# Four column products instead of six taps' worth: the last sample's convolution on one core

## The chip, the cores and the metric

The kernel runs on one core of a Trainium2 chip. The metric is the device time of one execution in microseconds (us), the median of several runs. Engines are named as the profile names them: PE (matrix products), DVE and POOL (element work), ACT (functions, scaling and copies), SP (it issues most of the DMAs). PE's results go to PSUM[...]; the other tiles lie in SBUF, and whole images between the layers lie in DRAM.

## The reference, cut to what matters

Four samples of 128 channels, 128 x 128 pixels, fp32, pass four residual layers. Each adds to its input a function of the group-normalised input: a deformable convolution, a dilated convolution, a state-space block with four scan directions, and at the end the layer that the change is about:

```python
def _L3_conv_ref(x, W, b):               # x: (4,128,128,128), W: (128,128,3,3)
    norm_out = conv3x3(x, W, padding=1) + b[None, :, None, None]
    s = jnp.sum(x, axis=1, keepdims=True)
    p = jnp.pad(s, ((0,0),(0,0),(1,1),(1,1)), mode='edge')
    diff = p[:,:,:-2,1:-1] + p[:,:,2:,1:-1] + p[:,:,1:-1,:-2] + p[:,:,1:-1,2:] - 4.0*s
    return norm_out - 0.7 * diff
...
x = x + _L3_conv_ref(_gn(x), L3_conv_W, L3_conv_b)
```

The second term is a Laplacian of the channel sum. Its taps can be added to the 3 x 3 taps; what differs is the image's edge, where the convolution pads with zeros and the Laplacian repeats the edge pixel.

## The kernel before, in words

The samples are pipelined. A long main loop, `scan`, goes through 4 samples x 4 directions x 32 blocks of four image rows; beside it a generator called `side` is pulled along in step and issues the other layers of the neighbouring samples. Both write into the same instruction stream, and `keep_order` fixes each engine's order to the order in which the program issued the instructions. `together` runs the scan and its side work; what is left of the side work when the scan ends is issued by `drain`. For the last sample, the rest of layer 2 (`layer2_post`) is such side work: its last blocks can come only when the scan has summed its last direction. Last of all, `drain(layer3(sts[last]))` issues the fourth layer of the last sample, with nothing beside it.

`weave(n, order)` is a software pipeline. `order` is a list of groups of (delay, step); in round t each step is issued for item t - delay, groups in the order of the list. A step that is a generator gives one instruction at a time, at its own place and at each `MORE`.

`layer3` works on the image in strips of 8 rows (SB) and blocks of 4 rows, 512 pixels (N). It loads the nine tap matrices (`w_l_sb`), changes five of them on DVE for the Laplacian (L1219, L1220), fills one matrix `edge` with -0.7, and computes the group normalisation's scale and shift (`gn_affine`: L214 to L226). Then per strip: SP fetches 10 rows (tile `xr`, L1234), ACT normalises them in two halves (`xn`, L1243); per block: PE adds nine matmuls of up to 512 columns into one bank, and one-column or one-row matmuls with `edge` at the image's edge (`p`, L1264); DVE adds bias and input (`o`, L1271); SP stores the block (L146). Two banks take turns. Each matmul of the program has two records in the trace.

`layer2_post` ends with a chain per block on PE, ACT and POOL (L1113 to L1179), the statistics on DVE (`bn_stats`, L1184) and the store of the block to the DRAM image `x3d`. It goes through the blocks from the bottom of the image to the top.

Every tile belongs to a pool with a number of buffers. When a tile's buffer is used again, the first instructions on the new tile wait for the last ones on the old. Pools are stacked from the left or the right end of SBUF. The scan's three pools (`sch`, `scb`, `scp`, right) stay open to the end of the kernel.

Of the kernel before, what the change touches and what calls it, by code (L numbers as in the profile page):

```python
# [10 lines left out]
F32 = mybir.dt.float32  # L11
I32 = mybir.dt.int32
U32 = mybir.dt.uint32
AF = mybir.ActivationFunctionType
ALU = mybir.AluOpType
# [3 lines left out]
P = 128  # L19
H = 128  # L20
W = 128
HW = H * W
R = 4
N = R * W
NBLK = H // R
KK = 9
# [10 lines left out]
THETA = 0.7  # L37
# [4 lines left out]
SB = 8  # L42
# [4 lines left out]
V_PREW, V_PREB, V_POSTW, V_POSTB, V_CONVB, V_ONW, V_ONB, V_B3 = range(8)  # L47
# [25 lines left out]
def keep_order(tc, started):  # L73

    last = {}
    for ins in tc.nc.cur_bb.bb.instructions[started:]:
        before = last.get(ins.engine)
        if before is not None:
            tc.add_manual_dep(
                ins,  # L80
                before,
                mybir.DependencyInfo(mybir.DependencyClass.NoSync, mybir.DependencyReason.DATA),
                reason="in order",
            )
        last[ins.engine] = ins.name
# [5 lines left out]
def weave(n, order, ready=lambda t: True):  # L91


    total = n + max(step[0] for group in order for step in group if step is not MORE)
    for t in range(total):
        while not ready(t):
            yield None
        left = iter(())
        for k, group in enumerate(order):
            for step in group:  # L100
                if step is MORE:
                    next(left, None)
                elif 0 <= t - step[0] < n:
                    more = step[1](t - step[0])
                    left = left if more is None else more
            yield (t + (k + 1) / len(order)) / total
        for _ in left:
            pass
# [3 lines left out]
def conv_preact_kernel(ctx: ExitStack, tc: tile.TileContext, a: dict, nb: int):  # L112
    nc = tc.nc
    x_in, out = a["x"], a["out"]
# [4 lines left out]
    pss = ctx.enter_context(tc.tile_pool(name="scps", bufs=1, space=PSUM))  # L119
    psb = ctx.enter_context(tc.tile_pool(name="bgps", bufs=1, space=PSUM))  # L120

    def load(pool, src, shape, name, **kw):
        t = pool.tile(shape, F32, name=name, **kw)
        nc.sync.dma_start(t, src)
        return t

    def bank(which, name):
        return psb.tile([P, N], F32, name=name, tag=f"bank{which}")

    waiting = []  # L130
    beside = {}

    def store(dst, src, after=3, of=None):

        waiting.append([after, of, dst, src])
# [4 lines left out]
    def tick():  # L140
        for w in waiting:
            w[0] -= 1
        due = [w for w in waiting if w[0] <= 0]
        waiting[:] = [w for w in waiting if w[0] > 0]
        for w in due:
            nc.sync.dma_start(*w[2:])  # L146

    def flush():
        while waiting:
            nc.sync.dma_start(*waiting.pop(0)[2:])  # L150
# [14 lines left out]
    def col(i):  # L165
        return vec[:, i : i + 1]
# [32 lines left out]
    def rows_of(t, y, n):  # L199

        return t[:, y * W : (y + n) * W].rearrange("p (r w) -> p r w", w=W)

    def flat(t):
        return t.rearrange("p r w -> p (r w)")

    def rsqrt(dst, src, eps):
        nc.scalar.activation(dst, src, AF.Ln, bias=eps)
        nc.scalar.activation(dst, dst, AF.Exp, scale=-0.5)

    def gn_affine(stats, which=0):  # L210

        both = bank(which, "pmv")
        mv = small.tile([P, 2], F32, name="mv")
        nc.vector.bn_aggr(mv, stats)  # L214
        pm = both[:, 0:1]
        nc.tensor.matmul(pm, gmat, mv[:, 0:1], start=True, stop=True)
        d = small.tile([P, 1], F32, name="gnd")
        nc.vector.tensor_sub(d, mv[:, 0:1], pm)
        e = small.tile([P, 1], F32, name="gne")
        nc.vector.scalar_tensor_tensor(e, d, d, mv[:, 1:2], ALU.mult, ALU.add)  # L220
        pv = both[:, 1:2]
        nc.tensor.matmul(pv, gmat, e, start=True, stop=True)
        sc = small.tile([P, 1], F32, name="gnscale")
        rsqrt(sc, pv, gn_eps)
        sh = small.tile([P, 1], F32, name="gnshift")
        nc.vector.scalar_tensor_tensor(sh, pm, -1.0, sc, ALU.mult, ALU.mult)  # L226
        return sc, sh
# [562 lines left out]

    def scan(pull):

        hp = ctx.enter_context(tc.tile_pool(name="sch", bufs=5, side="right"))
        bp = ctx.enter_context(tc.tile_pool(name="scb", bufs=2, side="right"))
        sp = ctx.enter_context(tc.tile_pool(name="scp", bufs=2, side="right"))
        seq = []
        for st in sts:
            for k in (0, 1, 3, 2):
                back = k >= 2
                order = reversed(range(NBLK)) if back else range(NBLK)  # L800
# [139 lines left out]
        def finish(t):  # L940
            st, k, i, back = seq[t]
            y = sp.tile([P, N], F32, name="y", bufs=1)
            nc.scalar.copy(y, blocks[t]["y"])
            store(blk(st["y"][k % 2], i), y, of=st["y"])
            blocks[t] = None
            st["summed"] = t % (NDIR * NBLK) + 1 - 3 * NBLK
# [33 lines left out]
        for t, (st, k, i, back) in enumerate(seq):  # L980
            c = blocks[t]
# [5 lines left out]
            for g in range(NG):  # L987
# [7 lines left out]
                h, n = c["h", g], NG - 1 if ready else NG  # L995
# [8 lines left out]
                at = t * NST + g * NG  # L1004
# [8 lines left out]
                for ng in range(NG):  # L1013
                    n = g * NG + ng
# [26 lines left out]
                    o, f = h[:, ng, :], c["a", n]  # L1041
                    if back:
                        o, f = o[:, ::-1], f[:, ::-1]
# [6 lines left out]
        t = len(seq) - 1  # L1050
# [4 lines left out]
        sums(t, 3, 1)  # L1055
        finish(t)
        flush()


    def layer2_post(st, engine=nc.gpsimd):  # L1060
# [150 lines left out]
    def layer3(st):  # L1211
        x3d, stats = st["x3"], st["stats3"]
        ob = out[st["b"]].rearrange("c h w -> c (h w)")
        with ExitStack() as s:
# [63 lines left out]
            yield from weave(NBLK, order)  # L1278
            flush()

    def chain(parts):

        total = sum(w for _, w in parts)
        done = 0.0
        for stage, w in parts:
            for f in stage:
                yield None if f is None else (done + w * f) / total
            done += w
# [20 lines left out]
    def drain(gen):  # L1309
        for _ in gen:  # L1310
            tick()

    def together(main, side, share):

        at = 0.0

        def pull():
            nonlocal at
            f = next(side, 1.0)
            at = at if f is None else f  # L1320
            return f is not None

        for f in main(pull):
            while at < f * share and pull():
                pass
            tick()
        drain(side)

    sts = [{"b": b} for b in range(nb)]
    last = nb - 1  # L1330

    def loads(engine, stage, spare=False):
        for f in stage:
            beside["busy"], beside["spare"] = engine, spare
            yield f
        beside["busy"], beside["spare"] = None, False

    def head(b):
        st = sts[b]
        table = [(loads(None, layer0_table(st), True), 12)] if b < 2 else []  # L1340
        return table + [(loads("POOL", layer0(st)), 28), (loads("PE", layer1(st), True), 14),
                (loads("PE", layer2_pre(st), True), 36)]

    def tail(b):
        load = "PE" if b + 1 < last else None
        engine = nc.vector if load else nc.gpsimd
        post, conv = loads(load, layer2_post(sts[b], engine), True), layer3(sts[b])
        if b + 2 > last:
            return [(post, 16), (loads(load, conv, True), 22)]
        return [(post, 16), (loads(load, abreast(conv, layer0_table(sts[b + 2])), True), 34)]  # L1350

    first = head(0)
    ahead = layer0_table(sts[0], False)
    for f in layer0(sts[0]):
        tick()
        for _ in range(3):
            next(ahead, None)
            tick()
    drain(chain(first[2:-1]))
    begun = rest(first[-1][0], lambda: sts[0].get("out", 0) >= 4)  # L1360

    def around(b):

        side = [(begun, 18)] if b == 0 else tail(b - 1)
        if b < last:
            return side + head(b + 1)
        load, rounds = sum(w for _, w in side), NBLK + 10
        side = [(stage, (NDIR * NBLK + LATE - rounds) * w / load) for stage, w in side]
        return side + [(loads(None, layer2_post(sts[b]), True), rounds)]

    over = 1 + LATE / (NDIR * NBLK)
    side = chain([(chain(around(b)), over if b == last else 1) for b in range(nb)])
    together(scan, side, nb / (nb - 1 + over))
    drain(layer3(sts[last]))
    keep_order(tc, started)


# [81 lines left out]
```

## Time and profile before

| | |
|---|---|
| median of 3 runs | 21988.68 us (21982.39 to 22019.09) |
| the profiled execution's own time | 22048.69 us |
| its span, first to last instruction | 22046.9 us |
| busy over the span: PE, DVE, ACT, POOL | 80%, 81%, 74%, 80% |
| scan loop's DVE scans (L1044) | 8192 of 1.267 us |
| last convolution's PE instructions (L1264) | 21780.3 to 22042.9 us |

A row of the profile's groups names the line of the kernel, the engine, the operation, output and input tiles with their shapes, the count, the busy time and mean length of one, and the idle time just before with what ended it. The shares of busy time over the span say little about a change to one stage; for that one asks for a stretch of time alone. In the timeline, `SPq` rows are DMAs being issued, and the length there is the issue, not the transfer. `PEld` are weight loads.

### The profile page before, as it was taken

To read this page: it belongs to the slowest core of one execution; us is meant where nothing else is said; L and a number is where in the kernel's file an instruction comes from. 1 tells how busy PE (TensorE), PEld (TensorE's weight loads), DVE (VectorE), ACT (ScalarE), POOL (GpSimd) and SP (SyncE) were. 2 spreads that over 40 slices of the span, in tenths; PEclk is the share of its full clock that TensorE was granted. 3 is DMA by queue.
4 is the path that set the end of the run, shared out by engine and by line. 5 is a ranking of instruction groups with operands and counts; after the bars stand their busy time and mean duration, and the time that the engine had idled before them with its cause. 6 is when DMAs were issued, how large, how long until landed. Compare 5 with 4: busy or idle time off the path is not lost. (4 is left out here: it accounts for less than half of the span.)

```text
span 22046.9 us, 206313 instructions
## 1 busy us (share of the span) xinstructions
PE 17530.0 (80%) x51536; PEld 8506.2 (39%) x51536; DVE 17759.7 (81%) x18759; ACT 16420.1 (74%) x37439; POOL 17657.2 (80%) x11985
## 2 busy tenths in 40 slices
PE   4667777888878888788888887887887878778788
PEld 3444333445323333454533333344543333233333
DVE  2332688888998899888798889978889888999984
ACT  4775777888778776788868876688877877666673
POOL 3663787667899999777789999977779999999994
PEclk7888998999989999999999999999999999999999
DMA  7666678777766878777776697777776677556674
GB/s 226 189 187 185 191 241 274 245 242 246 255 207 221 237 242 266 243 246 243 246 249 216 219 262 240 257 245 240 250 252 219 221 224 228 200 202 209 214 233 134
DMA packets 2578940, 5040.76 MB, mean 229 GB/s; under 512 B 1060736, under 2 KB 1333576, under 8 KB 2435408
## 3 DMA queue, kind: packets, MB, share of 16 engines
q1 hardware_dynamic: 2209104, 3819.31, 53.2%
q0 software_dynamic: 368640, 1208.25, 18.1%
q8 instruction: 415, 6.80, 0.1%
q14 instruction: 781, 6.40, 0.1%
HBM read 4082.03 MB, written 874.52 MB: 225 GB/s over the span
## 5 line engine op out<-in xcount | busy, mean ns | idle before, releaser
L1044 DVE TENSOR_TENSOR_SCAN h<-pa,carry,h 128x512 f32<-128x512 f32 x8192 | 10011.3, 1267 | 605.7 <-ACT pa L919 386.4
L933 PE MATMUL yacc<-h,gather_sb 128*128 128x512 f32 x15264 | 7958.5, 648 | 1906.5 <-POOL h L959 1303.9
L959 POOL TENSOR_TENSOR h<-h,cb 128x1024 f32<-128x1024 f32 x3651 | 8589.1, 2365 | 622.3 <-ACT carry L953 575.2
L426 POOL DMA_INDIRECT g<-table,idx x4608 | 4535.8, 984 | 2470.2 <-issue 1174.3
L919 ACT ACTIVATE pa<-spread,neg_a 128x512 f32<-128x512 f32 x8192 | 5488.6, 682 | 109.9 <-DVE h L1044 82.3
L933 PEld LDWEIGHTS yacc<-h,gather_sb 128*128 128x128 f32 x15264 | 2967.8, 206 | 6073.5 <-issue 2925.7
L996 DVE TENSOR_TENSOR h<-dub,bb 128x2048 f32<-128x2048 f32 (+1 forms) x2048 | 4210.4, 2056 | 519.8 <-ACT dub L893 517.4
L464 PE MATMUL pst<-ident,g 128*128 128x128 f32 x9216 | 2134.8, 319 | 1327.6 <-ACT smp L469 1097.8
L440 ACT ACTIVATE g<-g,wt 128x128 f32<-128x128 f32 x9216 | 2839.4, 390 | 42.1 <-DMA g<-table,idx 38.9
L953 ACT COPY carry<-h 128x2 f32<-128x2 f32 x4096 | 769.5, 188 | 2705.7 <-DVE h L1044 2699.4
L464 PEld LDWEIGHTS pst<-ident,g 128*128 128x128 f32 x9216 | 1686.8, 224 | 2174.2 <-ACT smp L469 1614.3
L465 PE MATMUL pst<-ident,v 128*128 128x128 f32 x9216 | 2129.5, 318 | 321.9 <-DVE v L454 170.8
L451 DVE TENSOR_TENSOR pw<-pw,g 128x512 f32<-128x512 f32 x1152 | 797.0, 692 | 1961.2 <-ACT pw L440 1555.4
L465 PEld LDWEIGHTS pst<-ident,v 128*128 128x128 f32 x9216 | 1674.8, 227 | 419.2 <-DVE v L454 225.0
L440 ACT ACTIVATE pw<-g,wt 128x128 f32<-128x128 f32 x4608 | 1691.8, 367 | 131.7 <-DVE v L454 11.4
L893 ACT COPY dub<-spread 128x512 f32<-128x512 f32 x2048 | 1195.7, 584 | 302.4 <-DVE h L996 111.8
L454 DVE SCALAR_TENSOR_TENSOR v<-g,wt,pw 128x128 f32<-128x128 f32 x4608 | 1293.6, 343 | 114.4 <-issue 2.3
L475 PE MATMUL acc<-smp,w_sb 128*128 128x512 f32 x2304 | 1287.6, 642 | 21.4 <-DVE x L482 14.8
L469 ACT COPY smp<-pst 128x512 f32<-128x512 f32 x1152 | 668.1, 580 | 776.3 <-remote 578.2
L1264 PE MATMUL p<-xn,w_l_sb 128*128 128x508 f32 (+2 forms) x2304 | 1129.7, 608 | 1.8 <-ACT xn L1243 1.8
L899 POOL TENSOR_TENSOR h<-spread,bb 128x512 f32<-128x512 f32 x845 | 1079.5, 1278 | 15.9 <-DMA spread<-stepsd 10.2
L872 POOL TENSOR_TENSOR e<-e,one_e 128x512 f32<-128x512 f32 x423 | 538.2, 1272 | 486.8 <-ACT one_e L856 463.7
(183 smaller groups left out, 18935.7 us busy)
## 6 DMA issues: line engine op xcount, KB each, us to landing
spread<-stepsd SPq DMA_DIRECT2D x2048, 512.0 KB
bb<-bcd SPq DMA_DIRECT2D x512, 1024.0 KB
cb<-bcd SPq DMA_DIRECT2D x512, 1024.0 KB
stepsd<-steps SPq DMA_DIRECT2D x512, 512.0 KB
table<-gt SPq DMA_DIRECT2D x512, 256.0 KB
g<-table,idx POOLq DMA_INDIRECT x4608
u<-urow SPq DMA_DIRECT2D x256, 256.0 KB
yrow<-y SPq DMA_DIRECT2D x256, 256.0 KB
```

The lines of the kernel that those rows point to most:

```text
L426: nc.gpsimd.indirect_dma_start(out=g[:, r].rearrange("p q c -> p (q c)"), out_offset=None, in_=table, in_offset=bass.IndirectOffsetOnAxis( ...
L440: nc.scalar.activation(pw[:, r * P : (r + 1) * P] if c == 0 else g[:, r, c, :], g[:, r, c, :], AF.Copy, scale=wv[:, r, q, k, c : c + 1],)
L454: nc.vector.scalar_tensor_tensor(v[:, r, :], g[:, r, 3, :], wv[:, r, q, k, 3:4], pw[:, r, :], ALU.mult, ALU.add)
L464: nc.tensor.matmul(dst, g[:, r, 2, :], ident, start=True, stop=False)
L465: nc.tensor.matmul(dst, v[:, r, :], ident, start=False, stop=True)
L475: nc.tensor.matmul(got["a", i], w0[:, k, :], got.pop(("c", n)), start=k == 0, stop=k == KK - 1)
L893: nc.scalar.copy(p, blocks[t]["p", g][:, 1, :])
L919: nc.scalar.activation(pa, blocks[t]["p", g][:, 0, :], AF.Exp, scale=neg_a[:, k, n : n + 1])
L933: nc.tensor.matmul(c["y"], gather[:, g, :], c["h", g][:, ng, :], start=g == 0 and ng == 0, stop=last and ng == parts[-1] and not second,)
L959: engine.tensor_mul(h, h, c["cb"][:, 2 * half : 2 * half + 2, :])
L996: nc.vector.tensor_tensor(h[:, 0:n, :], c["pdu", g].unsqueeze(1).to_broadcast([P, n, N]), c["bb"][:, 0:n, :], ALU.mult)
L1044: nc.vector.tensor_tensor_scan(o, f, o, carry[:, n : n + 1], ALU.mult, ALU.add)
```

## The change

A new generator `last_layers` takes the place of `layer2_post` in the last sample's side work, and calls it; the separate `drain(layer3(...))` at the end goes. For the samples before the last nothing changes.

The convolution of a row with three taps (a, b, c) is done for two neighbouring output columns at a time. From four neighbouring input columns c0 to c3 four operands are formed: c0 - c2, c1 + c2, c2 - c1 and c1 - c3. With the tap matrices a, (a + b + c)/2, (a - b + c)/2 and c they give four products m0 to m3, and the two output columns are m0 + m1 + m2 and m1 - m2 - m3. Each product is for half of the columns, so 512 columns of a matmul now cover 8 rows, and a strip takes 4 products x 3 row taps instead of 2 blocks x 9 taps.

In detail:

- The strips are taken from the bottom up (`r`), in rounds of a strip instead of a block.
- `prepare` loads the taps and forms the four kinds of matrices on DVE, once: at the first step of `layer2_post` after the scan has ended (`beside["over"]`, set in `together`). Its pool, and later the strips' pool, lie on the right, where the scan's pools are now closed at the scan's end (`held`).
- `frame` sets the border columns and rows of `xn` to zero on POOL; `xn` has W + 2 columns and three buffers.
- `mix` forms the operands: two sums on DVE, two differences on POOL, 640 columns each, reading every second column.
- `multiply` issues the products in the order 1, 2, 0, 3 into four banks; odd strips use the side work's four banks, even strips those that the scan has left. The edge matmuls go with products 0 and 3 (m3 enters with a minus, so its matrix has +0.7).
- `combine` copies m1 to SBUF on ACT, forms each of the two columns on DVE with two instructions (bias included), adds the input on POOL into every second column of `o3`, and stores the whole strip.

```diff
@@ -790,9 +790,10 @@
     def scan(pull):
-        hp = ctx.enter_context(tc.tile_pool(name="sch", bufs=5, side="right"))
-        bp = ctx.enter_context(tc.tile_pool(name="scb", bufs=2, side="right"))
-        sp = ctx.enter_context(tc.tile_pool(name="scp", bufs=2, side="right"))
+        held = ExitStack()
+        hp = held.enter_context(tc.tile_pool(name="sch", bufs=5, side="right"))
+        bp = held.enter_context(tc.tile_pool(name="scb", bufs=2, side="right"))
+        sp = held.enter_context(tc.tile_pool(name="scp", bufs=2, side="right"))
         seq = []
         for st in sts:
             for k in (0, 1, 3, 2):
@@ -1055,6 +1056,7 @@
         sums(t, 3, 1)
         finish(t)
         flush()
+        held.close()
     def layer2_post(st, engine=nc.gpsimd):
@@ -1278,6 +1280,132 @@
             yield from weave(NBLK, order)
             flush()
+    def last_layers(st):
+        NSTR, WH = H // SB, W // 2
+        with ExitStack() as s:
+            def prepare():
+                wp = s.enter_context(tc.tile_pool(name="l3w", bufs=1, side="right"))
+                w = load(wp, a["w_l3"], [P, KK, P], "w_l3_sb")
+                for t in (1, 3, 5, 7):
+                    nc.vector.tensor_scalar_add(w[:, t, :], w[:, t, :], -THETA)
+                nc.vector.tensor_scalar_add(w[:, 4, :], w[:, 4, :], 4.0 * THETA)
+                w4 = w.rearrange("p (y x) c -> p y x c", x=3)
+                outer, middle, mixed = w4[:, :, 0, :], w4[:, :, 1, :], []
+                both = wp.tile([P, 3, P], F32, name="both")
+                nc.vector.tensor_add(both, outer, w4[:, :, 2, :])
+                for op in (ALU.add, ALU.subtract):
+                    m = wp.tile([P, 3, P], F32, name=f"mixed{len(mixed)}")
+                    nc.vector.tensor_tensor(m, both, middle, op)
+                    nc.vector.tensor_scalar_mul(m, m, 0.5)
+                    mixed.append(m)
+                weights = (outer, mixed[0], mixed[1], w4[:, :, 2, :])
+                edges = []
+                for v in (-THETA, THETA):
+                    edges.append(wp.tile([P, P], F32, name=f"edge{len(edges)}"))
+                    nc.vector.memset(edges[-1], v)
+                return weights, edges
+            made = None
+            for f in layer2_post(st):
+                if made is None and beside.get("over"):
+                    made = prepare()
+                yield f
+            weights, edges = made or prepare()
+            x3d, ob = st["x3"], out[st["b"]].rearrange("c h w -> c (h w)")
+            pp = s.enter_context(tc.tile_pool(name="l3p", bufs=2, side="right"))
+            sc, sh = gn_affine(st["stats3"])
+            got = {}
+            def r(what):
+                return lambda n: what(NSTR - 1 - n)
+            def inside(j):
+                return (1 if j == 0 else 0), (SB + 1 if j == NSTR - 1 else SB + 2)
+            def fetch(j):
+                lo, hi = inside(j)
+                got["x", j] = xr = pp.tile([P, SB + 2, W], F32, name="xr3", bufs=5)
+                nc.sync.dma_start(xr[:, lo:hi, :], rows_of(x3d, j * SB - 1 + lo, hi - lo))
+            def frame(j):
+                got["n", j] = xn = pp.tile([P, SB + 2, W + 2], F32, name="xn3", bufs=3)
+                for x in (0, W + 1):
+                    nc.gpsimd.memset(xn[:, :, x : x + 1], 0.0)
+                lo, hi = inside(j)
+                for y in (*range(0, lo), *range(hi, SB + 2)):
+                    nc.gpsimd.memset(xn[:, y : y + 1, :], 0.0)
+            def normalise(part):
+                def one(j):
+                    lo, hi = inside(j)
+                    o = slice(lo, SB // 2) if part == 0 else slice(SB // 2, hi)
+                    nc.scalar.activation(
+                        got["n", j][:, o, 1 : W + 1], got["x", j][:, o, :], AF.Identity, bias=sh, scale=sc
+                    )
+                return one
+            def mix(j):
+                xn = got["n", j]
+                got["v", j] = v = pp.tile([P, 4, SB + 2, WH], F32, name="v3")
+                c = [xn[:, :, k : k + W - 1 : 2] for k in range(4)]
+                nc.vector.tensor_add(v[:, 1], c[1], c[2])
+                nc.vector.tensor_sub(v[:, 2], c[2], c[1])
+                nc.gpsimd.tensor_sub(v[:, 0], c[0], c[2])
+                nc.gpsimd.tensor_sub(v[:, 3], c[1], c[3])
+            def multiply(j):
+                xn, v = got.pop(("n", j)), got.pop(("v", j))
+                if j % 2:
+                    m = [bank(k, "m3") for k in range(4)]
+                else:
+                    m = [pss.tile([P, N], F32, name="m3", tag=tag, bufs=bufs)
+                         for tag, bufs in (("pa", 2), ("pa", 2), ("dub", 1), ("yacc", 1))]
+                got["m", j] = m
+                rows = slice(1, SB + 1)
+                for k in (1, 2, 0, 3):
+                    p = m[k].rearrange("p (r w) -> p r w", w=WH)
+                    jobs = [(p, weights[k][:, ty, :], v[:, k, ty : ty + SB, :]) for ty in range(3)]
+                    if k in (0, 3):
+                        e, x, first = (edges[0], 0, 1) if k == 0 else (edges[1], WH - 1, 2)
+                        at = 1 if k == 0 else W
+                        jobs.append((p[:, :, x : x + 1], e, xn[:, rows, at : at + 1]))
+                        for y, edge_row in ((0, 0), (SB - 1, H - 1)):
+                            if j * SB + y == edge_row:
+                                jobs.append((p[:, y, :], e, xn[:, 1 + y, first : first + W - 1 : 2]))
+                    for n, (dst, wt, src) in enumerate(jobs):
+                        nc.tensor.matmul(dst, wt, src, start=n == 0, stop=n == len(jobs) - 1)
+            def combine(j):
+                m, xr = got.pop(("m", j)), got.pop(("x", j))
+                s1 = pp.tile([P, N], F32, name="s3")
+                nc.scalar.copy(s1, m[1])
+                o = pp.tile([P, SB, W], F32, name="o3")
+                for x, op in ((0, ALU.add), (1, ALU.subtract)):
+                    e = pp.tile([P, N], F32, name=f"e{x}")
+                    nc.vector.tensor_tensor(e, s1, m[2], op)
+                    if x == 0:
+                        nc.vector.scalar_tensor_tensor(e, m[0], col(V_B3), e, ALU.add, ALU.add)
+                    else:
+                        nc.vector.scalar_tensor_tensor(e, e, col(V_B3), m[3], ALU.add, ALU.subtract)
+                    nc.gpsimd.tensor_add(
+                        o[:, :, x:W:2], e.rearrange("p (r w) -> p r w", w=WH), xr[:, 1 : SB + 1, x:W:2]
+                    )
+                store(ob[:, j * SB * W : (j + 1) * SB * W], flat(o), after=1)
+            order = [[(0, r(fetch)), (1, r(frame))], [(2, r(normalise(0)))], [(2, r(normalise(1)))],
+                     [(3, r(mix))], [(4, r(multiply))], [(4, r(combine))]]
+            for _ in weave(NSTR, order):
+                yield 1.0
+            flush()
     def chain(parts):
         total = sum(w for _, w in parts)
@@ -1324,6 +1452,7 @@
             while at < f * share and pull():
                 pass
             tick()
+        beside["over"] = True
         drain(side)
     sts = [{"b": b} for b in range(nb)]
@@ -1366,12 +1495,11 @@
             return side + head(b + 1)
         load, rounds = sum(w for _, w in side), NBLK + 10
         side = [(stage, (NDIR * NBLK + LATE - rounds) * w / load) for stage, w in side]
-        return side + [(loads(None, layer2_post(sts[b]), True), rounds)]
+        return side + [(loads(None, last_layers(sts[b]), True), rounds)]
     over = 1 + LATE / (NDIR * NBLK)
     side = chain([(chain(around(b)), over if b == last else 1) for b in range(nb)])
     together(scan, side, nb / (nb - 1 + over))
-    drain(layer3(sts[last]))
     keep_order(tc, started)
```

## The prediction, made before the result was known

> **What bounds the kernel now.** I read the page first, then asked the busy time of each engine in stretches of the last 350 us, because the diff touches only what runs behind the last scan block. In this view the columns are the stretch, its length, and busy time with instruction counts for PE, PEld, DVE, ACT and POOL, then the granted clock, the DMA share and GB/s.
>
> ```profile
> 21717.40:21780.30 62.90, 37.58 (x77) 13.78 (x75) 8.66 (x19) 38.18 (x63) 33.50 (x27) 0.88 0.46 157
> 21770.00:21780.30 10.30, 1.15 (x5) 1.01 (x5) 3.11 (x11) 1.44 (x4) 0.16 (x1) 0.50 0.78 268
> 21780.30:22042.90 262.60, 262.58 (x708) 125.62 (x708) 23.28 (x31) 26.30 (x31) 0.00 (x0) 0.99 0.19 63
> ```
>
> Up to 21717 the scan runs, then layer 2's last blocks finish, then 262.6 us belong to the last convolution. There PE is never idle, POOL does nothing, and DVE and ACT work a tenth of the time. The chain of waits agrees: start, length, engine and tile.
>
> ```profile
> 21770.68 3.69 DMA w_l_sb<-in_w_l_dram
> 21780.29 262.60 PE p L1264 x708
> ```
>
> So in this stage time is PE instructions, nothing else. Groups of the same window, shapes kept apart, say what one costs (busy us, mean ns):
>
> ```profile
> L1264 PE MATMUL p<-xn,w_l_sb 128*128 128x508 f32 x376 | 175.6, 589 | 0.0
> L1264 PE MATMUL p<-xn,w_l_sb 128*128 128x512 f32 x188 | 99.6, 611 | 1.8 <-ACT xn L1243 1.8
> L1264 PE MATMUL p<-xn,edge 128*128 128x4 f32 x128 | 16.1, 232 | 0.0
> ```
>
> Each matmul of the program leaves two records (576 for 288). The mean, 0.59 us, is latency, not spacing; successive weight loads in the timeline stand 0.427 us apart, so a 512-column matmul takes 0.854 us. The timeline (start, length) gives the block period and the way into the stage:
>
> ```profile
> 21770.20 0.70 DVE L1184 BATCH_NORM_STATS2 stats<-d 128x6 f32<-128x512 f32 x1 [2.71 <-POOL d L1179]
> 21770.68 0.34 SPq L124 DMA_DIRECT2D w_l_sb<-in_w_l_dram  x1
> 21774.78 0.79 DVE L1219 TENSOR_SCALAR w_l_sb<-w_l_sb 128x128 f32<-128x128 f32 x4 [3.89 <-DMA w_l_sb<-in_w_l_dram]
> 21775.76 0.96 DVE L214 BATCH_NORM_AGGREGATE mv<-stats 128x2 f32<-128x192 f32 x1
> 21779.08 0.16 DVE L226 SCALAR_TENSOR_TENSOR gnshift<-pmv,gnscale 128x1 f32<-128x1 f32 x1 [1.21 <-ACT gnscale L208]
> ...
> 21799.28 0.75 DVE L1271 SCALAR_TENSOR_TENSOR o<-p,vec_sb,xr 128x512 f32<-128x512 f32 x1 [7.28 <-PE p L1264]
> ...
> 21807.42 0.75 DVE L1271 SCALAR_TENSOR_TENSOR o<-p,vec_sb,xr 128x512 f32<-128x512 f32 x1 [7.38 <-PE p L1264]
> ...
> 22042.92 0.75 DVE L1271 SCALAR_TENSOR_TENSOR o<-p,vec_sb,xr 128x512 f32<-128x512 f32 x1 [7.07 <-PE p L1264]
> ```
>
> A block (4 rows) takes 21807.42 - 21799.28 = 8.13 us: nine matmuls, 18 x 0.427 = 7.69, and 0.44 for two edge matmuls of 4 columns, 0.11 us a record, the spacing of bare weight loads. 32 blocks make 260; the first was slow, 10.8 us against an expected 7.8, so 2.9 us of cold clock. The statistics wait on DVE behind the tap weights: ready at 21770.90, aggregated from 21775.76.
>
> For POOL and DVE, these groups of the whole run price the new element work:
>
> ```profile
> L959 POOL TENSOR_TENSOR h<-h,cb 128x1024 f32<-128x1024 f32 x3651 | 8589.1, 2365 | 622.3 <-ACT carry L953 575.2 <-DMA urow<-u 14.5 <-issue 8.3
> L876 POOL TENSOR_TENSOR steps<-steps,ln 128x512 f32<-128x512 f32 x423 | 542.9, 1283 | 0.3
> L959 DVE TENSOR_TENSOR h<-h,cb 128x1024 f32<-128x1024 f32 x445 | 561.3, 1261 | 5.4 <-ACT g L440 3.7 <-ACT carry L953 1.7
> ```
>
> POOL: (2365 - 1283)/512 = 2.11 ns an element over 0.2 us. DVE: 1.26 us for 1024, 0.67 to 0.75 us for 512 from PSUM (the last is L1271), so about 0.82 us for 640.
>
> [...] two DVE adds of 512 here (L961) took 2.72 us against 1.26 us for twice the elements[...]. No row here has that step; the nearest, the DVE transposing copy L772, took 1.59 us for 1024. [...] the pause stays, so the 2.9 us stay.
>
> **The change, part by part.**
>
> *Matmuls.* Before, a strip of 8 rows was two blocks: 18 full matmuls, 16.26 us with edges. After, it is 4 products x 3 row taps = 12 matmuls of 512 columns, 24 x 0.427 = 10.25 us, plus two edge matmuls (8 columns, one each in products 0 and 3, four exposed weight loads) 0.44: 10.69 us. 16 strips: 171.0. Image-edge rows: four matmuls of 64 columns, about 0.25 each, 1.0. Cold clock 2.9. Sum 174.9 against 262.6: **-87.7 us**.
>
> *New work under PE, per strip.* ACT: two halves of normalisation at 0.8 to 0.92 and one PSUM copy of 0.58, 2.4 us. DVE: two sums of 640 at 0.82, two PSUM sums at 0.69, two fused adds at 0.75: 4.5 us. POOL: two differences of 640 at 1.55, two output adds of 512 at 1.28, memsets about 0.4 (a guess; small memsets in this trace took 0.1 to 0.2): 6.1 us. All lie below 10.69. DMA: 640 KB in and 512 KB out per 10.69 us is 110 GB/s; this trace moved 268 in one stretch. Cover gone, the period becomes the longest of them.
>
> *The waits.* The xn3 tile has three buffers, and the frame of strip j+3 is issued before multiply(j); so POOL's memset waits for multiply(j) to end, and behind it on POOL stand both differences of strip j+1 and the output adds of strip j. Call that end T. Then product 0's operand is there at T+2.0, product 3's at T+3.5, the output adds end at T+6.1. PE issues products 1 and 2 first (5.1 us, from DVE sums made during the strip before), so 0 is needed at T+5.1, 3 at T+7.9. [...] The store waits on SP for POOL at T+6.1, and the fetch queued behind it is for a strip several ahead. PSUM alternates between two sets of four banks. PE should not stop. I take zero; bounds are -0 (PE cannot run under its own sum) and +3.6 a strip.
>
> *The way in.* Weight load and DVE preparation (about 3.3 us) move beside layer 2's last blocks, so aggregation starts at 21770.9, 4.86 earlier; the shift is there at 21774.4. The first fetch no longer stands behind the weights: issued about 21770.6, and landing like the weights (4.1 us for the same 576 KB) at 21774.9. Then two normalisation halves (1.73) and the first DVE sum (0.82) with about 0.1 of handover: first matmul 21777.6, 2.7 earlier than 21780.29. Against it, [...] the load is one more on SP: +1.0 taken, bounds 0 and +6. Should x3d's first fetch still wait for the last store (it did, 1.4 us), 2 us more. Net **-1.7**.
>
> *The way out.* Before, PE's last matmul to the span's end took 4.0 us. After it comes the DVE add 0.75, POOL's add 1.28 with handover, and a store of 512 KB instead of 256, which at 268 GB/s is 1 us more: 6.5 us. Net **+2.5**.
>
> Sum: -87.7 - 1.7 + 2.5 = -86.9. The profiled execution took 22048.69 (span 22046.9), so about 21962; the runs' median, 21988.68, lies 60 below that execution, and I take the difference over: 21988.7 - 86.9 = **21902 us**. The scan and everything before are issued in the same order; its pools close at its end, where nothing else waits for them.
>
> **The rivals.**
> 1. *The matmuls wait for the whole operand tile.* If products 1 and 2 too wait for POOL's two differences, PE stops 3.6 us in 15 strips: 54 us, time 21956. Against it: in the scan, POOL's L959 works on one half of tile h while DVE scans the other, so waits follow regions. 9 in 100.
> 2. *POOL becomes the bound.* If steps of two double its time, 12.2 a strip instead of 10.69, 16 x 1.5 = 24 lost, plus some start-up: 21929. For: no such row. Against: L772 above is only 1.26 times the price of a contiguous row. 8 in 100.
> 3. *Slower.* The same place and mechanism, harder: POOL passes strided pairs at over 2.6 times the price (5.6 ns an element). At that point the period is 10.69 + 87/16 = 16.1 us and the whole gain is gone; at three times, 18.3 us, the time is about 22024. Nothing in the trace speaks for it, but nothing measures it. 5 in 100.
> 4. *The sums aren't hidden in layer 2's tail*, or the first strip starts late, beyond my bounds: 21910 to 21925. 8 in 100.
> The forecast itself: 70 in 100.
>
> **How the numbers follow.** Apart from stalls the forecast is counted instructions at measured spacing; its own range is 21882 to 21922, mostly the spread of runs (three runs before lay 37 us apart). Two in ten may be left out: the range goes up past rivals 2 and 4, to 21948, and down to 21878. A measurement tells about 0.2%, 44 us, from no change: faster means under 21945. The forecast, rivals 2 and 4 are faster, 86 in 100; rival 1 mostly counts as the same, 8; slower 6.
>
> **What would show it.** Right: from the last layer 2 statistics on, a PE block of 170 to 178 us with strips 10.7 apart; POOL's add waits for PE at each frame; aggregation directly after the last statistics; no weight load in the chain. Wrong: PE idle inside strips with POOL or DVE as releaser, POOL differences longer than 2 us, or output adds that run into the next strip's differences.

## The result, and the profile after

The changed kernel takes 21923.32 us in the median of 8 runs (21916.58 to 21934.20), the kernel before 21992.93 in 8 (21982.39 to 22019.09): a ratio of 0.9967, 95% interval 0.9957 to 0.9977. That is 69.6 us less, where 86.9 were forecast (21902); 21923.3 lies one us above the forecast's own range (21882 to 21922) and inside the wider one (21878 to 21948). In a later comparison, where the kernel before took 22069.94 (8 runs), it took 21986.38 (5 runs): 83.6 less, ratio 0.9963 (0.9949 to 0.9978).

Up to the scan's end both programs issue the same instructions in the same order (37346 on ACT and 11958 on POOL in both traces), so I compare what comes after. Four stretches, read from the timeline of the profiled execution (span 21923.0): A, from the last group of the scan's sums on PE to the end of the last layer 2 statistics; B, to the convolution's first matmul; C, to the end of its last; D, to the end of the span.

| us | A | B | C | D | sum |
|---|---|---|---|---|---|
| before | 56.4 | 9.4 | 262.6 | 4.0 | 332.4 |
| after | 64.5 | 6.6 | 174.7 | 7.1 | 252.9 |
| difference | +8.1 | -2.8 | -87.9 | +3.1 | -79.5 |
| as predicted | +1.0 | -2.7 | -87.7 | +2.5 | -86.9 |

In the view by stretches of the changed kernel (stretch, length, busy time with counts of PE, PEld, DVE, ACT, POOL, granted clock, DMA share, GB/s) they are these rows:

```profile
21670.14:21734.60 64.46, 43.11 (x78) 15.63 (x78) 10.23 (x22) 36.62 (x59) 35.10 (x35) 0.87 0.35 119
21734.60:21741.16 6.56, 1.15 (x4) 1.00 (x4) 2.44 (x7) 3.06 (x6) 0.82 (x1) 0.50 0.99 359
21741.16:21915.87 174.71, 174.70 (x456) 81.73 (x456) 92.65 (x94) 34.10 (x45) 96.87 (x90) 0.99 0.27 93
21915.87:21923.00 7.13, 0.00 (x0) 0.00 (x0) 0.75 (x1) 0.00 (x0) 1.28 (x1) 0.69 0.18 74
```

PE is still never idle in C, with 456 records instead of 708; DVE and POOL now work half of that time under it. In the timeline the strips follow each other at 10.75 us, except the first (12.90, at a granted clock of 0.56 in its first 3.8 us) and the last (11.39). The groups of instructions, shapes kept apart (count, busy us, mean ns, idle time before):

```profile
L1384 PE MATMUL m<-v,w_l_sb 128*128 128x512 f32 x192 | 88.6, 599 | 0.0
L1384 PE MATMUL m<-v,mixed 128*128 128x512 f32 x192 | 88.0, 608 | 3.7 <-DVE v L1358 3.7
L1398 POOL TENSOR_TENSOR o<-e,xr 128x512 f32<-128x512 f32 x32 | 48.8, 1541 | 14.6 <-DVE e L1395 7.0 <-DVE e L1397 4.4 <-issue 3.2
L1359 DVE TENSOR_TENSOR v<-xn 128x640 f32<-128x640 f32 x16 | 29.1, 1817 | 0.0
L1361 POOL TENSOR_TENSOR v<-xn 128x640 f32<-128x640 f32 x16 | 28.4, 1776 | 0.0
L1358 DVE TENSOR_TENSOR v<-xn 128x640 f32<-128x640 f32 x16 | 23.2, 1451 | 2.1 <-ACT xn L1348 2.1
L1360 POOL TENSOR_TENSOR v<-xn 128x640 f32<-128x640 f32 x16 | 21.4, 1340 | 5.9 <-ACT xn L1348 5.9
```

PE waited for an operand once, before the first product (3.7 us). The element work is longer than the prices it was given (0.82 for each of DVE's two operands, 1.28 for POOL's adds). Beside each other both take longer: an operand of DVE took 0.83 us where it began just ahead of POOL's and 1.88 beside one of them; a difference on POOL took 1.26 ahead of DVE's and 1.85 beside them. No run tells why. It costs nothing here, since PE waits for none of it.

What went wrong lies in A. Before, layer 2's statistics and ACT's copy into the next of the four `d4` buffers came almost without delay, the copy 12.3 us after A's start:

```profile
21725.77 0.70 DVE L1184 BATCH_NORM_STATS2 stats<-d 128x6 f32<-128x512 f32 x1 [13.37 <-POOL d L1179]
...
21726.80 0.59 ACT L1158 COPY d<-pj 128x512 f32<-128x512 f32 x1 [1.04 <-DMA x3d<-d]
```

The same chain on the changed kernel's timeline (start, length):

```profile
21676.45 0.37 SPq L124 DMA_DIRECT2D w_l_sb<-in_w_l_dram  x1
21676.87 0.43 SPq L146 DMA_DIRECT2D x3d<-d  x1
...
21683.39 0.92 DVE L1292 TENSOR_SCALAR w_l_sb<-w_l_sb 128x128 f32<-128x128 f32 x4 [15.95 <-DMA w_l_sb<-in_w_l_dram]
...
21686.95 1.22 DVE L1186 BATCH_NORM_STATS2 stats<-d 128x6 f32<-128x512 f32 x2
21687.66 0.58 ACT L1160 COPY d<-pj 128x512 f32<-128x512 f32 x1 [6.28 <-DMA yl<-yd]
...
21691.05 2.08 PE L1167 MATMUL pv<-sq,jmat_sb 128*128 128x512 f32 x2 [5.75 <-ACT sq L207]
```

The load of the taps lands 6.9 us after its issue, not 4.1 as before; here it stands amid a burst of loads, five issued in the 2.4 us before it. DVE stands before the taps until then, works on them for 3.6 us, and only then comes to two blocks' statistics (L1186), the first of which could have started at 21681.3. ACT's copy, which needs the buffer that these statistics read, starts 0.07 us after the first of them ends (21687.59), 17.5 us after A's start. (The row names a load of `yl` as the end of its wait; but the products of `yl` that the copy reads were done by 21681.0, and `split` below confirms the statistics.) PE, idle 5.75 us, is slow afterwards: 2.08 us for a pair that took 1.12, at a granted clock of 0.50 from 21690 to 21694, against 0.99 in the four us before. So 5.2 of the 8.1 us are the copy's delay, and the rest goes with PE at the slow clock: it is busy 43.1 us in A, against 39.3 before.

### The profile page after: what moved, and what is told of

It is laid out like the page before. It is cut to its first block, busy times and chain, and to the rows that moved or that the text cites. A ratio compares the mean times of both kernels' runs of the same rounds, so it can differ in the third digit from the quotient of the medians.

```text
span 21923.0 us, 206062 instructions
## 1 busy us (share of the span) xinstructions
PE 17438.7 (80%) x51284; PEld 8443.2 (39%) x51284; DVE 17835.1 (81%) x18829; ACT 16424.9 (75%) x37455; POOL 17754.1 (81%) x12083
## 5 line engine op out<-in xcount | busy, mean ns | idle before, releaser
L1266 PE MATMUL p<-xn,w_l_sb 128*128 128x508 f32 (+2 forms) x1728 | 878.6, 615 | 0.0
```

## The experiments

Eight kernels ran, four on each of two chips. Since the time up to the scan's end differs by chip and by execution, they are compared by the four stretches of one profiled execution each; six of the eight ran only once. The edits are shown cut, and against the changed kernel unless said otherwise.

| us | A | B | C | D | sum |
|---|---|---|---|---|---|
| `late` | 56.4 | 13.3 | 175.4 | 7.1 | 252.1 |
| `split` | 60.4 | 6.5 | 175.8 | 7.1 | 249.8 |
| `split_later` | 56.4 | 6.5 | 175.3 | 7.1 | 245.3 |
| `old_taps_moved` | 61.2 | 6.5 | 261.3 | 4.0 | 332.9 |
| `pool_three` | 64.0 | 6.6 | 193.2 | 7.1 | 270.9 |
| `four_xn` | 64.5 | 6.4 | 174.7 | 7.1 | 252.7 |
| `all_three` | 57.2 | 8.0 | 173.2 | 7.0 | 245.4 |
| `after_again` | 64.5 | 6.6 | 174.6 | 7.1 | 252.9 |

### The same kernel again

No edit.

> The changed kernel, unaltered, on the same chip as the three above, to see how far the stretches repeat. Theory: A, B, C, D repeat within 1 us each (64.5, 6.6, 174.7, 7.1), while the time up to the scan's end, whose instructions are the same in every kernel here, differs by tens of us from run to run; the ratio to the kernel before is that of some 80 us. Rival: A's 64.5 was one execution's chance: it comes out below 60.

All four stretches repeat within 0.1 us, so 64.5 in A was no chance; `four_xn` and `pool_three`, with the same instructions in A, have 64.5 and 64.0. But C varies from 174.6 to 175.8 among kernels with the same instructions there, all of it in the first strip (12.8 to 14.0 us), and A of `all_three` is 0.8 above that of `split_later`. So a difference of about a microsecond in this table shows nothing by itself, and one of several does. The scan's last sums began at 21744.9 here, and at 21720.9, 21722.9 and 21715.3 in the three other kernels on this chip, with the same instructions up to there. With a spread of 30 us there, medians that differ by 69.6 in one comparison and 83.6 in the other agree with 79.5 in this part of the program; the 95% intervals, 51 to 95 and 49 to 113 us, hold it. On the other chip the time of the whole, one run each, would even call `pool_three` (21448.79) as quick as `late` (21449.15), though its stretches are 18.8 us longer.

### The taps prepared late, and the move alone

```diff
-                if made is None and beside.get("over"):
+                if False:
                     made = prepare()
```

> Only the place of the taps' load and of DVE's work on them is undone: both come after layer 2's last block again, before the group statistics; the four products stay. Four stretches are compared: A, from the scan's last group of sums on PE to the end of the last layer 2 statistics (56.4 us before, 64.5 us after the change); B, from there to the convolution's first matmul (9.4, 6.5); C, to the end of its last (262.6, 174.7); D, to the end of the span (4.0, 7.1). Theory: A grew because DVE stood waiting for the taps' load with layer 2's statistics queued behind it, and ACT then waited for the buffers that these free. Then A is 56 to 57, B grows to about 14 (load 4, taps 3.6, the rest as after), C and D stay: 252 in all, as after the change (253). Rival: A grew for another reason (a longer chain of the new program, chance): A stays above 62.

A falls to 56.4, what it was before the change, and B grows to 13.3: the growth of A came from loading and preparing the taps there. On the timeline of `late` the price in B is to be read:

```profile
21251.28 0.38 SPq L124 DMA_DIRECT2D w_l_sb<-in_w_l_dram  x1
...
21255.49 0.63 DVE L1292 TENSOR_SCALAR w_l_sb<-w_l_sb 128x128 f32<-128x128 f32 x4 [3.92 <-DMA w_l_sb<-in_w_l_dram]
...
21258.77 0.96 DVE L214 BATCH_NORM_AGGREGATE mv<-stats 128x2 f32<-128x192 f32 x1
```

With one store ahead of it and the strips' fetches behind it the load lands in 4.2 us; load and taps stand 7.2 us before the group statistics. With the four products and without the move, the stretches are 0.8 us shorter than with both: A wins what B loses, and the move as it was made gains nothing. The other half, the move with the nine taps of before (here against the kernel before; the scan's pools are closed at its end, as in the change):

```diff
-            w = load(wp, a["w_l3"], [P, KK, P], "w_l3_sb")      # in layer3, after layer2_post
-            ... DVE's work on five taps, edge
+            for f in layer2_post(st):
+                if made is None and beside.get("over"):
+                    made = prepare()                            # the same load and work
+                yield f
```

> The move alone: the nine-tap convolution of before, with its taps' load and DVE's work on them (1.2 us instead of 3.6) beside layer 2's end, where the change has them. Theory: A grows less than with the change's longer DVE work, to 59 to 62; B shrinks to about 7; C 262.6 and D 4.0 stay: 333 to 336, nothing won against before (332). Rival, the prediction's own account (1 us lost in A, 2.7 won in B): 330.5.

A +4.8, B -2.9, C -1.3: nothing won against before (332.9 and 332.4), as expected. C is shorter by the first block alone (9.44 us, 10.76 before): PE's single weight loads take 0.33 or 0.34 us up to 2.5 us after the first matmul and 0.19 behind that, where before they took as much up to 5.7 us after it (granted clock 0.72 from 3.7 to 7.7 us). The products alone give -80.3 (`late` against before), the move alone +0.5; together they make -79.8, and -79.5 was measured. The two parts add up.

### The load and DVE's work apart

```diff
+                if taps_in and made is None:
+                    later += 1
+                    if later == 36:
+                        made = prepare(*taps_in)      # DVE's work; the load stays where it was
```

> The load of the taps stays where the change puts it; DVE's work on them comes 36 steps (a bit over two blocks) later. Theory: with the load landed by then, DVE never stands, A is 56 to 58, B stays at 6.5, C 174.7, D 7.1: 245 in all, 8 less than after the change. Rivals: the load's share of the DMA engines delays layer 2 (A stays at 62 or more, with DMAs as releasers)[...].

Half of the loss went: 60.4. Neither reading was right alone. DVE's work still stood 1.55 us for the load, but the statistics were ahead of it and nothing waited behind it; the timeline of `split` names another wait:

```profile
21225.01 0.69 DVE L1186 BATCH_NORM_STATS2 stats<-d 128x6 f32<-128x512 f32 x1 [13.36 <-POOL d L1181]
...
21227.26 0.68 DVE L1294 TENSOR_SCALAR w_l_sb<-w_l_sb 128x128 f32<-128x128 f32 x4 [1.55 <-DMA w_l_sb<-in_w_l_dram]
...
21227.94 0.58 ACT L1160 COPY d<-pj 128x512 f32<-128x512 f32 x1 [2.92 <-DMA x3d<-d]
```

The buffer that ACT copies into is free when its last content has also been stored to `x3d`, and that store was issued right behind the taps' load, at 21220.51: the copy starts 7.4 us after the store's issue, where it was 6.0 before. In the next kernel the load too comes later, behind the burst:

```diff
+                later += bool(beside.get("over"))
+                if later == 36:
+                    taps_in = fetch_taps()
+                if later == 68:
+                    made = prepare(*taps_in)
```

> The taps' load is issued 36 steps after the scan's end, behind layer 2's burst of loads, and DVE's work on the taps 32 steps after that. Theory: of the 8.1 us by which A grew, about half was DVE standing for the load (split took 4.1 off) and half the load's share of the DMA queues, which made a buffer's store to x3d land late; with both gone A is 56 to 57.5, B 6.5, C and D as after: 244 to 246. Rival: the rest of the 4 us is [...] a longer chain: A stays at 59 to 61.

A is 56.4, to the tenth what it was before the change, with the taps still prepared beside layer 2. The same copy on this timeline:

```profile
21735.01 0.59 ACT L1160 COPY d<-pj 128x512 f32<-128x512 f32 x1 [0.85 <-DMA x3d<-d]
...
21736.27 0.34 SPq L124 DMA_DIRECT2D w_l_sb<-in_w_l_dram  x1
```

So the 8.1 us were two things of about 4 each, taken off one after the other: the order in DVE's queue, and the taps' load ahead of the store. Each made PE pause and then run slower: of A's single weight loads, otherwise 0.19 to 0.21 us, 8 took 0.29 to 0.34 in the changed kernel (granted clock in A 0.87), 7 took 0.33 or 0.34 in `split`, and none did in `split_later` and before (0.95). No run tells whether the store lost time by its place behind the load or by sharing the DMA engines with it. DVE's 3.6 us of work cost nothing once they stood elsewhere, though four of its instructions took 2.16 us there, beside POOL at work, and 0.79 in the kernel before.

### How much cover POOL's work has

```diff
-                nc.gpsimd.tensor_sub(v[:, 0], c[0], c[2])
+                for _ in range(3):
+                    nc.gpsimd.tensor_sub(v[:, 0], c[0], c[2])      # v[:, 3] likewise
```

> Each of POOL's two differences is computed three times in every strip. As read from the profile after the change, a strip costs POOL 1.34 + 1.78 for the differences, 2 x 1.54 for the output adds and 0.16 for the frame, 6.4 us; with three times the differences about 12.6, above PE's 10.7. Theory: POOL becomes the bound, strips 12.6 to 13 us apart, C about 174.7 + 15 x 2.1 = 206, and PE waits for POOL within strips. Rival: PE already waits for part of POOL's work somewhere, then the whole 6.2 us of extra work show: strips 16 to 17 us, C about 265.

C grew by 18.5, not by 31. The groups of `pool_three` say why the price was too high, and what waits:

```profile
L1386 PE MATMUL m<-v,w_l_sb 128*128 128x512 f32 x192 | 90.5, 607 | 12.8 <-POOL v L1363 12.7 <-POOL v L1361 0.2
L1361 POOL TENSOR_TENSOR v<-xn 128x640 f32<-128x640 f32 x48 | 75.4, 1571 | 8.4 <-ACT xn L1348 5.9
L1363 POOL TENSOR_TENSOR v<-xn 128x640 f32<-128x640 f32 x48 | 61.1, 1273 | 2.5
L1400 POOL TENSOR_TENSOR o<-e,xr 128x512 f32<-128x512 f32 x32 | 40.5, 1289 | 1.1 <-DVE e L1399 1.1
```

Two rows of its timeline:

```profile
21353.95 2.84 PE L1386 MATMUL m<-v,w_l_sb 128*128 128x512 f32 x6 [0.94 <-POOL v L1363]
...
21357.04 0.15 POOL L1339 MEMSET xn<- 128x10 f32 x2 [0.64 <-PE m L1386]
```

Here a difference for product 3 takes 1.27 us and an output add 1.29; the means of the profile after (1.78, and 1.54) held time beside DVE's operand sums (1.85 us a difference, up to 1.87 an output add); here these instructions come after the sums. PE's rounds of products 1 and 2 start 12.01 us apart (21344.76, 21356.77), against 10.75 after. PE waits before product 3 (12.7 us in all); before product 0 it waits 0.2 us, before 1 and 2 not at all after the first strip. POOL is not full either: it works 11.06 of the 12.01 us, and its frame waits 0.64 us for PE. What sets the period is a ring: the frame waits for the end of the strip's products, because `xn` has three buffers; behind it come the six differences (8.8 us), behind these PE's product 3 (2.8), and then the next frame; the output adds run beside product 3. This is read from the timeline; no run gave these differences a fourth buffer. Three times the differences is a little too much; once leaves POOL over 4 us a strip free.

```diff
-                got["n", j] = xn = pp.tile([P, SB + 2, W + 2], F32, name="xn3", bufs=3)
+                got["n", j] = xn = pp.tile([P, SB + 2, W + 2], F32, name="xn3", bufs=4)
```

> The normalised strip's tile xn3 gets four buffers instead of three, so POOL's frame of a strip no longer waits for the products three strips before. Theory, as predicted: that wait is hidden, PE is bound by its own instructions: C stays at 174.7 to 176, the whole from the scan's end at 250 to 254; only POOL's wait for PE in front of the memsets goes or moves. Rival: some product waits for POOL's place in its order: C falls by 2 or more.

POOL's frame, in the changed kernel and then in `four_xn`:

```profile
L1339 POOL MEMSET xn<- 128x10 f32 x26 | 2.1, 116 | 64.1 <-PE m L1384 63.9 <-issue 0.2
```

```profile
L1339 POOL MEMSET xn<- 128x10 f32 x26 | 1.9, 113 | 0.0
```

The wait of 64 us is gone and C is the same to the hundredth (174.70, 174.71). In the changed kernel it was hidden.

### A version with more

On top of `split_later`: the last strip's second column finished and stored in halves, and three matmuls of constants ahead of the first product, where the changed kernel has PE at a granted clock of 0.56 for 3.8 us and at 1.00 for the next four.

```diff
+            for n in range(3):
+                nc.tensor.matmul(warm, jmat, gather.rearrange("p g c -> p (g c)"), start=n == 0, stop=n == 2)
...
-                store(ob[:, j * SB * W : (j + 1) * SB * W], flat(o), after=1)
+                    for h in range(parts):      # 2 for x == 1 of the last strip: add, add, store of half the rows
```

> The taps' load and DVE's work as in split_later; the last strip's second column is finished and stored in two halves; three matmuls of constants into a free bank run on PE while the first strip is fetched and normalised. Expected: A 56 to 57.5; B 6.5; C 172 to 173 (the clock is up when the products start; 2.9 us of cold clock at most to win); D 5.2 to 5.7 instead of 7.1: 240.5 to 243 from the scan's end, 10 to 12 less than the changed kernel. Rival: the clock's start isn't moved by three matmuls, or they delay the first product: C stays at 175 or B grows.

Both additions missed. Timeline of `all_three`:

```profile
21775.21 5.47 PE L1329 MATMUL warm<-gather_sb,jmat_sb 128*128 128x512 f32 x6
...
21778.09 0.83 DVE L1367 TENSOR_TENSOR v<-xn 128x640 f32<-128x640 f32 x1 [2.01 <-ACT xn L1357]
...
21780.47 5.60 PE L1393 MATMUL m<-v,mixed 128*128 128x512 f32 x12
```

The three matmuls ran slow themselves (their single weight loads took 0.34 us, as at the granted clock of 0.50 in the changed kernel's A, and 0.19 only from 0.7 us after the first product's start) and were in the way: the operand was ready at 21778.9, the first product began at 21780.5. Against `split_later` C is 2.1 us shorter, all of it in the first strip (11.43, 13.53), but B is 1.5 longer and A 0.8. In D the transfer ended 0.7 us sooner after the last matmul, but the program's end came only 0.1 sooner. The median of its runs is 21961.64 us (21953.75 to 21975.23, 4 runs), ratio to the kernel before 0.9952 (0.9935 to 0.9969); the changed kernel on the same chip stood at 0.9963, so the intervals overlap. Of the 24.7 us between the two medians the stretches show 7.5, all of it `split_later`'s; the rest lies before the scan's end, and nothing explains it. By the stretches `split_later`, the simpler of the two, is as good.

## Why the prediction was right, and where it wasn't

**The matmuls**: 174.9 predicted, 174.7 measured, strips 10.75 us apart for 10.69. Counting instructions at their spacing (0.427 us a record, 0.11 for exposed weight loads) was enough, because nothing else came to the path. That it fits to 0.2 us is luck: 16 strips at 10.75 cost 1.0 more than forecast, and the slow clock at the start and the image's edge rows 1.2 less (2.7 for 3.9). That the 2.9 us of slow clock of the one trace of before would come again was my own estimate; the first strips of the kernels here (12.8 to 14.0 us) show that it varies by over a microsecond.

**The new work under PE**: right that it is hidden, with reserve. The reasoning on POOL's wait for a buffer held: hidden as the change stands (`four_xn`), and a link of the ring once the differences are three times as long (`pool_three`). There the period is not the longest engine's sum, as the prediction had it for the case that cover runs out: it is 12.01 us where POOL works 11.06. The price of 1.55 us for a difference was high (1.26 to 1.27), though its mean in the changed kernel, up to 1.78, seems to say the contrary: there most of those for product 3 ran beside DVE's operand sums, at 1.85 us.

**The way in**: -2.7 predicted for the first matmul, -2.8 measured; the first fetch's landing was the last wait, as said, and the normalisation began 4.0 us after the last statistics, as computed. The counter-item failed: "the load is one more on SP: +1.0 taken, bounds 0 and +6". It was +8.1, above even the upper bound. I had priced what the preparation does, about 3.3 us of DVE and one load more on SP, and not what stands behind it in its queues: the statistics behind a DVE that waits for a load, and the store to x3d behind the load, both of which free the buffers of the chain that sets A's end. The prediction asked who is queued behind a waiting instruction on POOL and SP, and didn't ask it for DVE. It also took the landing time (4.1 us; 6.9 came) from a load with only a store ahead of it.

**The way out**: +2.5 predicted, +3.1 measured; a size only. The store is the term: from its issue to the span's end 5.0 us for 512 KB and 3.2 for 256, so 1.8 more, where 1.0 was taken.

**The rest** of the gap, 79.5 in the profiled executions against 69.6 in the medians, lies before the scan's end, among identical instructions. That it is chance is argued from the 30 us of spread there, from the intervals and from the 83.6 of the later comparison; nothing took it apart further.

**The rivals**: rival 1 (products wait for the whole operand tile) is out: in `pool_three` product 0 started while POOL was still at product 3's operand. Rivals 2 and 3 (POOL as the bound) didn't come: that a step of two costs no more had been my own estimate, and the differences at that step took 1.26 to 1.27 us for 640 elements, against the 1.28 of L876 for 512. At the lengths that POOL's instructions have away from DVE's operand sums, its work of a strip is 2 x 1.27 + 2 x 1.29 + 0.16 = 5.3 us against PE's 10.75. Rival 4, the preparation not hidden, is what happened: A went 7 us beyond the estimate, and the measured 21923.3 lies in that rival's span (21910 to 21925). So the main term was right by its mechanism; that the sum stayed in the wider range, in spite of A, is owed to a range that had been widened for this rival.

## What to carry to other kernels

Moving a load and its work to a stage with idle engines is not free because the engines are idle. Here the first instruction on the loaded tile stood in DVE's queue until the load landed, 6.9 us after its issue, with two blocks' statistics behind it; and the copy that waits for the store issued behind the load started 7.4 us after that store's issue, 6.0 before (`split`). Each cost about 4 us. Ask what short instruction or store is queued behind and which buffers it frees, issue the load behind the stage's own burst and the work two rounds later; here that was worth 7.6 us of the stretches. Before counting a longer mean of an instruction as its price, see whether another engine works beside it: the difference for product 3 had a mean of 1.78 us beside DVE's operand sums, and of 1.27 in `pool_three`, where it came after them. And where an engine waits for another's buffers, reckon the reserve along that ring, not by each engine's sum (12.01 us a strip in `pool_three`, where POOL works 11.06).

## What the runs showed of the hardware

- POOL took 1.26 to 1.27 us for a difference of 640 elements with both inputs read at a step of two from one tile, as much as for 512 elements at a step of one from two tiles (1.28). No run tells why.
- The kernel before, the same instructions each time, took 21542.89 us on one chip (one run), 22069.94 on another (8 runs) and 21992.93 in the first comparison (8 runs). Its stretches were traced once only; those of the other kernels don't follow the chip (`late` on the first has A 56.4 and C 175.4, `split_later` on the second 56.4 and 175.3).
- After PE had stood idle for 5.75 us in A of the changed kernel, its granted clock was 0.50 for the next 3 us of its work; behind the pause at the start of C, kernels with the same instructions took 12.8 to 14.0 us for the first strip.
- With the last strip's store cut in two halves the transfer ended 0.7 us sooner after the last matmul, and the program only 0.1 us sooner (one trace of each).
